# Reciprocal roots of the heads' variances: from three Newton steps on VectorE and GpSimd to logarithm, exponential and one Newton step

## The chip, the cores and the metric

The kernel runs on one core of one Trainium2 chip. The metric is the device time of one execution in microseconds (us), the median over several runs. The engines are TensorE (PE in the profile; PEld are its weight loads), VectorE (DVE), ScalarE (ACT), GpSimd (POOL) and SyncE (SP, which here only issues DMAs). An engine executes its own instructions in order and waits for the others by semaphores.

## The reference

Two layers act on x, of 4 batches x 256 tokens x 256 features. A layer is a gated cross attention to a context of 1601 tokens x 128 features, followed by a gated feed-forward part. The change lies in the attention of the first layer, which has 16 heads of 16 features. Queries and keys are normalised head by head before the scores:

```python
def _ln(t, w, b):
    m = jnp.mean(t, axis=-1, keepdims=True)
    v = jnp.var(t, axis=-1, keepdims=True)
    return (t - m) * jax.lax.rsqrt(v + EPS) * w + b

q = _ln((x @ Wq + bq).reshape(b, s1, H, HD), qn_w, qn_b)
k = _ln(kv[..., :HD], kn_w, kn_b)
ctx = _attn(qT, k, v) + _attn(qT, k_dca, v_dca)   # softmax over 1585 keys, and over the last 16 apart
x = x + jnp.tanh(g_xattn[0]) * (ctx @ Wo + bo)
```

So each token has one reciprocal root per head: 16 for a key token, 16 for a query token. The last 16 context tokens are a group of keys with norm weights of their own. The feed-forward part is a mixture of 16 experts in the first layer, and one with ternary weights in the second. They and the second attention aren't touched.

## The kernel before, in words

**Tiling.** Tokens lie on the 128 partitions. The 1585 main keys are 13 tiles of 128 tokens, prepared in five groups (three tiles each, the last of one). A group's keys are `kn`, 128 x 48 heads x 16 features; a batch's queries are `qraw`, 128 x 32 heads x 16. A variance tile has one column per head: 48, 32 or 16 of them.

**Preparing a group of keys.** `key_project` multiplies context by weights (L475); VectorE adds the bias into `kn` (L477), ScalarE copies the values into `vp` (L478). The mean is removed beforehand by centring the weights and biases (`center`). `scale_heads` then gives three steps: `square` on ScalarE (L379), `rsqrt`, and `scale`, in which GpSimd multiplies `kn` by the root (L388). `rsqrt` sums the squares and adds the epsilon on VectorE (L382, L383), makes a first guess with two integer instructions there (L365, L366), and runs three Newton steps of four instructions each on GpSimd (`pool_rsqrt`, L368 to L371), with the square's own buffer `sq` as work space. Then `split` writes the result as a sum of three bf16 parts: ScalarE rounds (L345, L349), GpSimd subtracts for keys and VectorE for queries (L346, L350). Last, SP transposes the parts into `kT` (L520). Queries go the same way, with their norm weights applied on VectorE (L544 to L551) and staged by GpSimd for each quarter of the heads (L616, L619).

**The loop.** A batch is four slabs of four heads, a slab is 14 slots. In each slot TensorE makes scores for the maxima (L647), whose maximum VectorE takes (L654), scores for the exponentials (L686), which ScalarE takes (L694), and multiplies with the values (L708). Between these, `plan_keys` and `plan_queries` place the steps of preparing the next batch at fixed slots: a step placed at slot n comes after the slot's own instructions on every engine. A group that begins at slot s has its square at s, `rsqrt` at s+1, `scale` at s+3, the two halves of the split at s+4 and s+6 and the transposes at s+7. This is done for batches 1, 2 and 3 while the batch before is attended to: 15 groups of keys and 3 of queries, 18 calls of `scale_heads`.

**The setup.** The first batch is prepared before the loop, with three larger roots in `deviations` (L829): two groups of keys and the queries together (128 columns), the rest of the keys (112), and the last tokens (16). They use `newton_rsqrt`, all on VectorE: two integer instructions (L356, L357) and three Newton steps of three (L359 to L361). The keys of this batch are in `kT`'s second buffer (`kn0`), multiplied by their root at L855.

**Order.** `keep_order` fixes the order of the instructions on each engine to the one in which they are written, so nothing moves past a waiting instruction.

Of the kernel before, what the change touches and what calls it, by code (L numbers as in the profile page):

```python
# [9 lines left out]
F32 = mybir.dt.float32  # L10
BF16 = mybir.dt.bfloat16
I32 = mybir.dt.int32
# [9 lines left out]
P = 128  # L22
# [26 lines left out]
def bc_last(ap, n):  # L49

    return ap.unsqueeze(2).to_broadcast([ap.shape[0], ap.shape[1], n])
# [8 lines left out]
def tile_gated_cross_blocks(ctx: ExitStack, tc: tile.TileContext, a: dict, out: bass.AP):  # L60
# [202 lines left out]
    with ExitStack() as ph:  # L263
# [12 lines left out]
        def load_group(b, gi):  # L276
# [4 lines left out]
            nc.sync.dma_start(out=t[:, :n], in_=a["ctxT"][:, b, k0 : k0 + n])  # L281
            return t

        wkv = wp.tile([P, 2 * D], F32, name="wkv")
        bkv = wp.tile([P, 2 * D], F32, name="bkv")
        nc.sync.dma_start(out=wkv[:, :D], in_=a["L0_xattn_Wk"])
# [64 lines left out]

            return [first, second]

        def newton_rsqrt(v, y, t):

            nc.vector.tensor_scalar(y.bitcast(I32), v.bitcast(I32), 1, None, ALU.arith_shift_right)  # L356
            nc.vector.tensor_scalar(y.bitcast(I32), y.bitcast(I32), -1.0, 1597463007.0, ALU.mult, ALU.add)  # L357
            for k in range(3):
                nc.vector.tensor_tensor(t, y, y, ALU.mult)  # L359
                nc.vector.scalar_tensor_tensor(t, t, -0.5, v, ALU.mult, ALU.mult)  # L360
                nc.vector.scalar_tensor_tensor(v if k == 2 else y, t, 1.5, y, ALU.add, ALU.mult)  # L361

        def pool_rsqrt(v, y, t):

            nc.vector.tensor_scalar(y.bitcast(I32), v.bitcast(I32), 1, None, ALU.arith_shift_right)  # L365
            nc.vector.tensor_scalar(y.bitcast(I32), y.bitcast(I32), -1.0, 1597463007.0, ALU.mult, ALU.add)  # L366
            for k in range(3):
                nc.gpsimd.tensor_tensor(t, y, y, ALU.mult)  # L368
                nc.gpsimd.tensor_tensor(t, t, v, ALU.mult)
                nc.gpsimd.tensor_scalar(t, t, -0.5, 1.5, ALU.mult, ALU.add)  # L370
                nc.gpsimd.tensor_tensor(v if k == 2 else y, t, y, ALU.mult)  # L371

        def scale_heads(src, n, g):

            sq = hp.tile([P, GN * H, HD0], F32, name="sq", bufs=1)
            v = small.tile([P, GN * H], F32, name="hn_var", bufs=2)[:n, :g]

            def square():
                nc.scalar.activation(sq[:n, :g], src, AF.Square)  # L379

            def rsqrt():
                nc.vector.reduce_sum(v, sq[:n, :g], axis=AX.X)  # L382
                nc.vector.tensor_scalar(v, v, 1.0 / HD0, 1e-6, ALU.mult, ALU.add)  # L383
                space = sq.rearrange("p g e -> p (g e)")[:n]
                pool_rsqrt(v, space[:, :g], space[:, g : 2 * g])

            def scale():
                nc.gpsimd.tensor_tensor(src, src, bc_last(v, HD0), ALU.mult)  # L388

            return [square, rsqrt, scale]  # L390


        bmask = wp.tile([P, HG], F32, name="bmask")
# [376 lines left out]
        def plan_keys(plan, b, base, at, l):  # L770

            ctxg, kns = {}, {}
            for gi, g in enumerate(groups):

                def fetch(gi=gi):
                    ctxg[gi] = fetched.pop((b, gi), None) or load_group(b, gi)

                place(plan, base + max(at[0][0], at[gi][0] - 8), [fetch])
                for i, slot in enumerate(at[gi]):
                    place(plan, base + slot, [lambda gi=gi, i=i: key_project(b, gi, ctxg[gi], kns, i)])  # L780

                def begin(gi=gi, slot=base + l[gi]):
                    steps = key_parts(gi, kns)
                    steps[0]()
                    for o, step in zip((1, 3, 4, 6), steps[1:]):
                        place(plan, slot + o, [step])
                    place(plan, slot + 7, [lambda: key_turn(b, gi)])

                place(plan, base + l[gi], [begin])
# [37 lines left out]
        def deviations(c0, c1):  # L827
            v = v0[:, c0:c1]
            nc.vector.tensor_scalar(v, v, 1.0 / HD0, 1e-6, ALU.mult, ALU.add)  # L829
            y, t = (lp.tile([P, NKT * H], F32, name=f"nr_{k}")[:, : c1 - c0] for k in "yt")  # L830
            newton_rsqrt(v, y, t)

        def square(t0, t1, base):

# [61 lines left out]
        first_pair(6, kn0)  # L896
        step(group[0])
        nc.vector.tensor_tensor(q3, q3, bc_last(v0[:, qcol : qcol + QT * H], HD0), ALU.mult)
        affine, fold, first_split, second_split = query_parts(0)[3:]
        affine()  # L900
        first_pair(8, kn0)
        step(group[0])
# [43 lines left out]
        for _ in last:  # L946
            pass
        nc.scalar.activation(gate, gate, AF.Tanh)
        early.close()
        ep = ph.enter_context(tc.tile_pool(name="l0e", bufs=4))  # L950

# [17 lines left out]
        for u, (b, s) in enumerate(slabs):  # L969
# [3 lines left out]
            if s == 0 and b + 1 < B:  # L973
                plan_keys(plan, b + 1, base_slot, KEYS[b > 0], PARTS_AT[b > 0])
                iterate(plan, base_slot + 32, last_tokens(b + 1), 12)
                if b == 0:
                    plan_queries(plan, 1, base_slot, [0, 3, 9, 10], [13, 14], [15, 16, 18, 19, 20, 21, 23])
                if b + 2 < B:
                    plan_queries(
                        plan, b + 2, base_slot + NS * SLOTS, [-8, -6, -4, -3], [-2, -1], [0, 1, 3, 4, 6, 8, 10]  # L980
                    )
            if s == 0 and b > 0:

# [665 lines left out]
```

## Time and profile before

| | |
|---|---|
| Median of 3 runs | 1640.45 us (1640.38 to 1642.27) |
| Profiled execution: its time, its span | 1644.6 us, 1642.8 us |
| PE busy | 1542.2 us (94%) |
| DVE busy | 1170.4 us (71%) |
| ACT busy | 788.0 us (48%) |
| POOL busy | 658.1 us (40%) |
| Chain that ended last, by engine | PE 77%, DVE 13%, ACT 3%, issue 2%, POOL 2% |
| Mean granted TensorE clock | 0.976 |

The span is the time from the first to the last instruction of one profiled execution; the table's shares are of that. The stages are: setup to 89 us, the first attention with preparation of the next batch to 492 us, its last batch to 603 us, and everything else (experts, second attention, second feed-forward part) after. A line of the groups has source line, engine, operation, output and inputs, shapes, count, busy time and mean duration, then the idle time of the engine ahead of them and who ended it. A line of the timeline has start and duration in us.

### The profile page before, as it was taken

To read this page: it belongs to the slowest core of one execution; us is meant where nothing else is said; L and a number is where in the kernel's file an instruction comes from. 1 tells how busy PE (TensorE), PEld (TensorE's weight loads), DVE (VectorE), ACT (ScalarE), POOL (GpSimd) and SP (SyncE) were. 2 spreads that over 40 slices of the span, in tenths; PEclk is the share of its full clock that TensorE was granted. 3 is DMA by queue.
4 is the path that set the end of the run, shared out by engine and by line. 5 is a ranking of instruction groups with operands and counts; after the bars stand their busy time and mean duration, and the time that the engine had idled before them with its cause. 6 is when DMAs were issued, how large, how long until landed. Compare 5 with 4: busy or idle time off the path is not lost.

```text
span 1642.8 us, 34188 instructions
## 1 busy us (share of the span) xinstructions
PE 1542.2 (94%) x13274; PEld 924.6 (56%) x13282; DVE 1170.4 (71%) x2621; ACT 788.0 (48%) x1808; POOL 658.1 (40%) x754
## 2 busy tenths in 40 slices
PE   4598899899999999998999999999999999999998
PEld 1254454454455554445666666666666666666665
DVE  6876668767767736677777777777877777877655
ACT  2144545554555553453555444544455444454443
POOL 4534414513621215534445444444445444444410
PEclk8699899999999999999999999999999999999999
DMA  3512612430424132000000000010000000000000
GB/s 102 100 35 45 94 32 45 78 57 16 87 44 95 37 90 110 1 2 2 15 9 21 9 15 15 8 21 3 15 9 15 15 15 15 9 2 2 2 0 27
DMA packets 148466, 54.06 MB, mean 33 GB/s; under 512 B 133200, under 2 KB 143952, under 8 KB 148176
## 3 DMA queue, kind: packets, MB, share of 16 engines
q1 hardware_dynamic: 134592, 50.65, 14.6%
q10 hardware_dynamic: 13712, 1.23, 0.6%
q8 instruction: 104, 1.70, 0.4%
q14 instruction: 58, 0.48, 0.1%
HBM read 24.30 MB, written 1.05 MB: 15 GB/s over the span
## 4 chain that ended last, share of the span: by engine, by line
PE 77%; DVE 13%; ACT 3%; issue 2%; POOL 2%; DMA 1%; ACTq 0%; SPq 0%; DVEq 0%; POOLq 0%
PE ps_o L1426 21%; PE ps_sc L1363 20%; PE ps_s L686 6%; PE ps_s L647 6%; PE ps_o L708 5%; DVE mxs L654 4%; PE ps_y L1444 4%; PE ps_m L1352 3%; PE ps_m L475 2%; PE ps_v L1186 2%; ACT pr L1378 1%; PE ps_a L1200 1%; PE ps_g L1557 1%; PE ps_x L1131 1%; PE ps_y L1582 1%
## 5 line engine op out<-in xcount | busy, mean ns | idle before, releaser
L1413 POOL TENSOR_TENSOR pr<-pr,rs 128x1604 f32<-128x1604 f32 x128 | 364.2, 2867 | 434.9 <-DMA rs<-ws 393.2
L1426 PE MATMUL ps_o<-pT,cx 128*128 128x256 f32 x1664 | 372.2, 381 | 7.8 <-DVE pT L1419 7.8
L1370 DVE CUSTOM_DVE_ANT_0 pr<-ps_sc,mk 128x401 f32<-128x401 f32 x512 | 294.6, 576 | 95.0 <-PE ps_sc L1363 56.2
L1363 PE MATMUL ps_sc<-ctxT,qT 128*32 128x401 f32 x4096 | 359.5, 502 | 0.4 <-DVE nm L1370 0.4
L1378 ACT ACTIVATE pr<-pr,nm 128x401 f32<-128x401 f32 x512 | 321.3, 629 | 71.0 <-DVE nm L1370 70.3
L1426 PEld LDWEIGHTS ps_o<-pT,cx 128*128 128x128 f32 x1664 | 318.0, 191 | 52.2 <-DVE pT L1419 8.5
L654 DVE TENSOR_REDUCE mxs<-ps_s 128x2 f32<-128x768 f32 (+1 forms) x256 | 245.9, 979 | 78.5 <-PE ps_s L647 77.9
L694 ACT ACTIVATE e<-ps_s 128x1024 f32<-128x1024 f32 (+1 forms) x224 | 214.7, 963 | 176.0 <-PE ps_s L686 161.5
L1419 DVE STREAM_TRANSPOSE pT<-pr 128x1664 f32<-128x1664 f32 x128 | 242.9, 1899 | 4.9 <-POOL pr L1413 4.7
L1363 PEld LDWEIGHTS ps_sc<-ctxT,qT 128*32 128x32 f32 x4096 | 126.2, 110 | 204.4 <-issue 119.5
L647 PE MATMUL ps_s<-kT,qTs 64*128 64x384 bf16 (+1 forms) x1536 | 177.6, 346 | 40.4 <-DMA qTs<-qp 18.1
L686 PE MATMUL ps_s<-qTs,kT 64*128 64x256 bf16 x2496 | 176.1, 272 | 11.0 <-DVE mxs L654 11.0
L686 PEld LDWEIGHTS <-kT 64*128 64x128 bf16 x2496 | 125.8, 95 | 57.5 <-issue 23.6
L647 PEld LDWEIGHTS <-qTs 64*128 64x128 bf16 x1536 | 67.0, 97 | 138.4 <-issue 91.4
L708 PE MATMUL ps_o<-e,vp 128*32 128x256 f32 x1664 | 112.8, 390 | 0.0
L1395 ACT ACTIVATE ws<-ws 32x32 f32<-32x32 f32 x64 | 14.6, 228 | 194.3 <-DVE ws L1394 194.3
L1436 ACT COPY ao<-ps_o 128x256 f32<-128x256 f32 x64 | 23.9, 373 | 152.5 <-PE ps_o L1426 141.3
L1378 ACT ACTIVATION_READ_ACCUMULATOR pr<-pr,nm 128x1 f32 x512 | 95.4, 186 | 0.0
L1444 PE MATMUL ps_y<-vo,ao 128*128 128x256 f32 x256 | 73.3, 409 | 2.1 <-ACT ao L1436 2.1
L1444 PEld LDWEIGHTS ps_y<-vo,ao 128*128 128x128 f32 x256 | 43.9, 191 | 46.5 <-ACT pr L1378 39.9
L708 PEld LDWEIGHTS ps_o<-e,vp 128*32 128x32 f32 x1664 | 44.6, 110 | 43.0 <-issue 25.6
L1352 PE MATMUL ps_m<-xnT,aq 128*128 128x256 f32 x256 | 65.8, 380 | 0.0
(288 smaller groups left out, 1553.9 us busy)
## 6 DMA issues: line engine op xcount, KB each, us to landing
ctxT<-in_ctxT_dram SPq DMA_DIRECT2D x4, 800.5 KB, 8.0
ctxg<-in_ctxT_dram SPq DMA_DIRECT2D x16, 192.0 KB, 3.2
kT<-in_L_xattn_Wq_dram SPq DMA_DIRECT2D x4, 512.0 KB, 3.5
wo<-in_L_xattn_Wo_dram SPq DMA_DIRECT2D x4, 512.0 KB, 4.5
bq<-nm SPq DMA_DIRECT2D x128, 2.0 KB, 1.7
bq<-nm ACTq DMA_DIRECT2D x128, 2.0 KB, 2.0
rs<-ws SPq DMA_DIRECT2D x128, 1.0 KB, 1.9
rs<-ws ACTq DMA_DIRECT2D x128, 1.0 KB, 1.8
```

The source lines that it names most:

```text
L647: nc.tensor.matmul(ps[:, k, :w], lhsT=qT[rows, j, i, r, :], rhs=kT[rows, 2 * s + r, c0 : c0 + w], start=j == 0, stop=j == NP - 1,)
L654: nc.vector.tensor_reduce(greatest_of[u][:, i, 2 * r : 2 * r + 2, n], ps[:, :, :w], AX.X, ALU.max)
L686: nc.tensor.matmul(ps[:, k, jj * S : (jj + 1) * S].rearrange("p (i q) -> p i q", i=QT), lhsT=kT[rows, 2 * s + r // 2, (j + jj) * P : (j + ...
L694: nc.scalar.activation(e[:, :, : nj * S], ps[:, :, : nj * S], AF.Exp)
L708: nc.tensor.matmul(summed[u][(r + k) * W : (r + k + 1) * W, :S], lhsT=vps[b % 2][:, j + jj, h * VW : h * VW + W], rhs=made[u, j, r][:, k, ...
L1363: nc.tensor.matmul(ps[i * TQ : (i + 1) * TQ, :KS], lhsT=queries[u][:, t * TQ : (t + 1) * TQ], rhs=ctxT[b][:, i * KS : (i + 1) * KS], start ...
L1370: nc.vector.tensor_tensor_reduce(out=prs[u % 3][:, t, :KS], in0=ps[:, :KS], in1=masks[b], scale=-1.0, scalar=3.0e38, op0=ALU.add, op1=ALU. ...
L1378: nc.scalar.activation(p, p, AF.Exp, bias=found[u][:, 0, t : t + 1], scale=-1.0, accum_out=found[u][:, 1, t : t + 1])
L1413: nc.gpsimd.tensor_tensor(p, p, bc_last(factors[:, ts], KS), ALU.mult)
L1419: nc.vector.transpose(pTs[u % 2][:, ts].rearrange("p t k -> p (t k)"), prs[u % 3][:, ts].rearrange("p t k -> p (t k)"))
L1426: nc.tensor.matmul(po[:, u % 2], lhsT=contexts[b][:, k, :], rhs=pTs[u % 2].rearrange("p t (k q) -> p t k q", q=TQ)[:, :, k, :], start=k == ...
L1444: nc.tensor.matmul(ys[b][:, i], lhsT=outs[u][:, i * P : (i + 1) * P], rhs=vo[:, h, :], start=(h, i) == (0, 0), stop=(h, i) == (H - 1, QT - 1),
```

## The change

The root becomes `exp(-0.5 * ln(v))` on ScalarE (`log_root`, two instructions), with one Newton step on VectorE after it (`newton`, three instructions). Both older helpers go. In `scale_heads` the step `rsqrt` is divided: `variance` at slot s+1 on VectorE, `root` at s+2 on ScalarE, and the Newton step at s+3 ahead of GpSimd's multiply. The work space is now two small tiles of their own, `hn_y` and `hn_t`, with one buffer each. ScalarE loads a table set that has both functions at the start of the program, and again after Tanh.

```diff
+        nc.scalar.preload_act_table_set("natural_log_exp_and_others")
         wkv = wp.tile([P, 2 * D], F32, name="wkv")
         bkv = wp.tile([P, 2 * D], F32, name="bkv")
         nc.sync.dma_start(out=wkv[:, :D], in_=a["L0_xattn_Wk"])
...
-        def newton_rsqrt(v, y, t):
-
-            nc.vector.tensor_scalar(y.bitcast(I32), v.bitcast(I32), 1, None, ALU.arith_shift_right)
-            nc.vector.tensor_scalar(y.bitcast(I32), y.bitcast(I32), -1.0, 1597463007.0, ALU.mult, ALU.add)
-            for k in range(3):
-                nc.vector.tensor_tensor(t, y, y, ALU.mult)
-                nc.vector.scalar_tensor_tensor(t, t, -0.5, v, ALU.mult, ALU.mult)
-                nc.vector.scalar_tensor_tensor(v if k == 2 else y, t, 1.5, y, ALU.add, ALU.mult)
-
-        def pool_rsqrt(v, y, t):
-
-            nc.vector.tensor_scalar(y.bitcast(I32), v.bitcast(I32), 1, None, ALU.arith_shift_right)
-            nc.vector.tensor_scalar(y.bitcast(I32), y.bitcast(I32), -1.0, 1597463007.0, ALU.mult, ALU.add)
-            for k in range(3):
-                nc.gpsimd.tensor_tensor(t, y, y, ALU.mult)
-                nc.gpsimd.tensor_tensor(t, t, v, ALU.mult)
-                nc.gpsimd.tensor_scalar(t, t, -0.5, 1.5, ALU.mult, ALU.add)
-                nc.gpsimd.tensor_tensor(v if k == 2 else y, t, y, ALU.mult)
+        def log_root(v, y):
+
+            nc.scalar.activation(y, v, AF.Ln)
+            nc.scalar.activation(y, y, AF.Exp, scale=-0.5)
+
+        def newton(v, y, t):
+
+            nc.vector.tensor_tensor(t, y, y, ALU.mult)
+            nc.vector.scalar_tensor_tensor(t, t, -0.5, v, ALU.mult, ALU.mult)
+            nc.vector.scalar_tensor_tensor(v, t, 1.5, y, ALU.add, ALU.mult)
 
         def scale_heads(src, n, g):
...
+            y, t = (small.tile([P, GN * H], F32, name=f"hn_{k}", bufs=1)[:n, :g] for k in "yt")
...
-            def rsqrt():
+            def variance():
                 nc.vector.reduce_sum(v, sq[:n, :g], axis=AX.X)
                 nc.vector.tensor_scalar(v, v, 1.0 / HD0, 1e-6, ALU.mult, ALU.add)
-                space = sq.rearrange("p g e -> p (g e)")[:n]
-                pool_rsqrt(v, space[:, :g], space[:, g : 2 * g])
+
+            def root():
+                log_root(v, y)
 
             def scale():
+                newton(v, y, t)
                 nc.gpsimd.tensor_tensor(src, src, bc_last(v, HD0), ALU.mult)
 
-            return [square, rsqrt, scale]
+            return [square, variance, root, scale]
...
-                    for o, step in zip((1, 3, 4, 6), steps[1:]):
+                    for o, step in zip((1, 2, 3, 4, 6), steps[1:]):
                         place(plan, slot + o, [step])
...
             y, t = (lp.tile([P, NKT * H], F32, name=f"nr_{k}")[:, : c1 - c0] for k in "yt")
-            newton_rsqrt(v, y, t)
+            log_root(v, y)
+            newton(v, y, t)
...
         nc.scalar.activation(gate, gate, AF.Tanh)
+        nc.scalar.preload_act_table_set("natural_log_exp_and_others")
...
-                    plan_queries(plan, 1, base_slot, [0, 3, 9, 10], [13, 14], [15, 16, 18, 19, 20, 21, 23])
+                    plan_queries(plan, 1, base_slot, [0, 3, 9, 10], [13, 14], [15, 16, 17, 18, 19, 20, 21, 23])
...
-                        plan, b + 2, base_slot + NS * SLOTS, [-8, -6, -4, -3], [-2, -1], [0, 1, 3, 4, 6, 8, 10]
+                        plan, b + 2, base_slot + NS * SLOTS, [-8, -6, -4, -3], [-2, -1], [0, 1, 2, 3, 4, 6, 8, 10]
```

One further line in the setup takes the queries' later steps from the fifth place of the list on, not the fourth.

More of the change, by code (lines that the diff above doesn't have):

```diff
@@ L898, in tile_gated_cross_blocks @@
         nc.vector.tensor_tensor(q3, q3, bc_last(v0[:, qcol : qcol + QT * H], HD0), ALU.mult)
-        affine, fold, first_split, second_split = query_parts(0)[3:]
+        affine, fold, first_split, second_split = query_parts(0)[4:]
         affine()
```

## The prediction

> **What bounds the kernel now.** I read the busy row and the chain that ended last first (TensorE 94% of the span, 77% of the chain), then cut the span by stage. The windows view, columns length, then busy time of PE, PEld, DVE, ACT, POOL, then granted clock, shows that the part the change touches isn't one regime:
>
> ```profile
> 23.50:50.30 26.80, 6.13 (x26) 2.15 (x25) 21.29 (x38) 7.96 (x12) 13.03 (x13) 0.64 0.33 60
> 50.30:68.20 17.90, 8.36 (x52) 3.98 (x50) 14.51 (x29) 4.53 (x7) 12.91 (x22) 0.69 0.61 98
> 89.00:218.00 129.00, 116.94 (x1310) 62.37 (x1312) 87.14 (x161) 68.15 (x100) 48.69 (x116) 0.95 0.31 52
> 492.00:603.00 111.00, 108.84 (x1546) 66.10 (x1542) 64.83 (x144) 63.30 (x78) 17.96 (x42) 1.00 0.29 68
> ```
>
> Until 89 us VectorE sets the pace (21.3 busy of 26.8). From 89 to 492 us, the loop in which the next batch's keys and queries are prepared, TensorE does, but is idle 33 of 403 us; from 492 us, where no keys are prepared, it is idle 2.2 of 111. What the change can win in the loop lies in those 33 us. After 603 us nothing it touches runs.
>
> The timeline of the setup has the first root. It stands on the chain with VectorE alone; ScalarE is idle from 21.69 to 27.63, GpSimd until 27.15:
>
> ```profile
> 23.31 0.23 DVE L829 TENSOR_SCALAR v<-v 128x128 f32<-128x128 f32 x1
> 23.57 0.23 DVE L356 TENSOR_SCALAR nr_y<-v 128x128 int32<-128x128 int32 x1
> ...
> 26.38 0.29 DVE L360 SCALAR_TENSOR_TENSOR nr_t<-nr_t,v 128x128 f32<-128x128 f32 x1
> 26.70 0.29 DVE L361 SCALAR_TENSOR_TENSOR v<-nr_t,nr_y 128x128 f32<-128x128 f32 x1
> ...
> 27.15 3.39 POOL L855 TENSOR_TENSOR kT<-kT,v 128x768 f32<-128x768 f32 x2 [14.78 <-DVE v L361]
> ```
>
> In the loop I listed every wait of TensorE and followed its releaser back. The longest, with brackets giving the idle time and who ended it:
>
> ```profile
> 161.14 0.29 POOL L371 TENSOR_TENSOR hn_var<-sq 128x48 f32<-128x48 f32 x1
> 161.36 0.21 POOL L616 MEMSET qp<- 128x24 bf16 x1
> 161.42 1.80 POOL L619 COPY qp<-qn 128x192 bf16<-128x192 bf16 x6
> 163.17 1.64 POOL L350 TENSOR_TENSOR kp<-kn,kp 128x768 bf16<-128x768 f32 x1
> ...
> 164.85 0.42 DVE L477 TENSOR_TENSOR kn<-ps_m,bkv 128x256 f32<-128x256 f32 x1 [5.74 <-POOL kp L350]
> ...
> 165.31 0.37 ACT L478 COPY vp<-ps_m 128x256 f32<-128x256 f32 x1 [5.97 <-DVE kn L477]
> ...
> 165.73 2.08 PE L475 MATMUL ps_m<-wkv,ctxg 128*128 128x512 f32 x2 [3.62 <-ACT vp L478]
> ```
>
> GpSimd's twelve root steps (157.30 to 161.43) hold back the split at L350, that the buffer `kn`, that VectorE, ScalarE and TensorE. The wait costs twice: the granted clock is 0.50 from 166 to 170 us and 0.73 from 170 to 172, so two matmuls of L475 take 2.08 instead of 1.12.
>
> **The change part by part.** ACT prices come from ACTIVATE rows: 228 ns at 32 columns, 408 at 256, so 0.8 ns a column: 241 ns at 48, 292 at 112, 305 at 128. A Newton instruction takes 0.29 at 128 columns and 0.17 at 16 (start to start 0.33 and 0.21), so at 48 about 0.24.
>
> *Setup roots.* At 128 columns eleven instructions, 23.57 to 26.99 (3.4 us), become two ACT and three DVE: 2 x 0.305 + 3 x 0.33 + three hand-overs of 0.03 = 1.7. Saved 1.7. VectorE's next instruction stands behind the Newton step and waits with it. The 112-column root (47.00 to 50.26) goes from 3.3 to 1.6: saved 1.7, ScalarE being idle from 45.18. The 16-column root (65.49 to 68.21) saves 1.6 of VectorE's time and nothing of the span: at 71.24 TensorE waits for the transposed `kp_last`, queued on SP behind six transposes of about 1.4 us issued from 59.3 on, and VectorE was itself only 0.33 us from waiting for it. Setup: -3.4.
>
> *Table loads.* The load moves from 9.76 us, where it followed ScalarE's DMA issues, to ahead of them, so these go out 1.3 us later. `wkv` then lands at 4.9, not 3.6; centring it takes 1.1 and is done before `x` lands at 7.5. The bias is centred at 8.8 and its transfer was issued by 2.2; the first copy of ScalarE starts at 11.06 either way. Cost 0; 1.3 if the cover fails, -0.5 if the `x` tiles land earlier without this traffic. The two loads around Tanh (2 x 1.283) lie in ScalarE's 13.36 us of idle before its first L694. Here a rule speaks against the change: the Trainium skill, "ScalarE: Activation LUTs", section "What ACT_TABLE_LOAD costs", adds a drain of about 1380 ns, 2.66 us a switch. The trace has the copy 0.02 us after its load (9.76 + 1.28, then 11.06), no drain. By the rule the pair costs 5.3, still inside the idle time, and the first transfers go out 2.7 late: `wkv` is centred at 7.4, still in time, and the first copy is 1.4 late. I take the row.
>
> *Loop.* Eighteen calls of `scale_heads`. GpSimd loses L368 to L371, 13.7 + 14.6 + 12.6 + 9.7 + 4.9 = 55.5 us. VectorE loses two integer steps (0.45 a call) and gains three (0.72): +0.27 a call, 4.9 in all. ScalarE gains 0.5 a call, 9. Moved: the multiply L388 followed GpSimd's chain as soon as that ended; now it waits for the Newton step two slots after the variance. A slot is 403/176 = 2.3 us, so it comes about as late as after the old chain (3.9 to 4.2 us). Behind the new waits: the logarithm waits for the variance issued a slot earlier, with the next slots' exponentials L694 behind it; Newton waits for ScalarE with the maxima L654 behind it. Each has a slot of lead. The ledger of TensorE's waits:
>
> - 165.73, 3.62: L350 needs only the copy ending at 158.35 and the staging, so it starts near 158.6, not 163.2; wait gone. Clock loss of 5.4 us at half speed gone too. -6.3.
> - 313.20 and 452.18, 1.78 each: ScalarE waits for L388, which stood behind GpSimd's roots, layernorm and staging. Without the roots it starts near 308, not 309.87. -1.8 each, -3.6.
> - 261.02 and 397.12, 2.8 each: VectorE's L549 took 1.98 instead of 0.67 while L388 ran (below). L388 now follows a Newton step that stands after L549. -1.3 each, and half of the 2.9 of half-speed clock that follows the second: -4.0.
> - 294.64 and 433.60, 1.0 each: L668 took 1.33 instead of 0.17 under L388, which moves behind it. -2.0.
> - 188.26, 2.34: one link is ScalarE's square waiting 1.37 for GpSimd. About -1.0, and half its 1.7 of slow clock: -1.8.
> - 148.74: 0.45 of integer steps less in front. -0.3.
>
> Sum -18.0. I give back a quarter (4.5), since engines that catch up show the wait behind, and charge a quarter (3.5) of the 13.9 us added to VectorE and ScalarE, as both are idle over a quarter of the loop; if all of it reached TensorE it would be 13.9. Loop: -10.0.
>
> The second rule that speaks against: "SBUF — State Buffer", section "SBUF: two separate sides": a VectorE instruction with two SBUF inputs and a GpSimd instruction reading SBUF exclude each other for a whole instruction. The trace agrees:
>
> ```profile
> 256.22 1.56 POOL L388 TENSOR_TENSOR kn<-kn,hn_var 128x768 f32<-128x768 f32 x1
> 256.34 1.98 DVE L549 TENSOR_TENSOR kb<-qraw,bc_L_xattn_kn_b 128x512 f32<-128x512 f32 x1
> ```
>
> L549 ends 0.54 us after L388. All three Newton instructions have two SBUF inputs, so a call that meets a GpSimd pass (1.5 to 1.65) can wait that long; at 48 columns by the row alone it is 0.72, by row and lock up to 2.4. In the order of the steps only the last group of the first prepared batch has such a pass in its slot; I add nothing beyond the charge.
>
> **Total.** -3.4 + 0 - 10.0 = -13.4. Against the profiled execution (span 1642.8, its time 1644.6) that is 1631.2; the median of the runs is 1640.45, 4 lower, which gives 1627.0. Bounds: -21.4 with nothing given back or charged (1619), -1.7 with the quarter given back, all added work on the path and a late start (-3.4 + 1.3 - 13.5 + 13.9: 1638.8).
>
> **The rivals.**
>
> - *Only the setup gains.* The waits are refilled by what stands behind them, since TensorE also waits for the maxima L654 13.3 us in sum in the loop. For: VectorE gains work. Against: the longest waits have GpSimd as their link. 1640.45 - 3.4 = 1637.0.
> - *All of it, and more clock.* Ledger in full: about 1619. For: the batch of 358.9 to 494.3 repeats the one before and took 2.9 us longer through one clock drop. Against: after a removed wait comes the next.
> - *The lock decides.* Newton meets GpSimd passes call after call, VectorE is late with L654 and TensorE waits. At 1.65 a hit and -13.4 - 3.5 otherwise, it needs more than ten hits in 18 that reach TensorE; with 15 the time is 1640.45 - 16.9 + 24.8 = 1648. Against: L350 of a group lies three slots behind its Newton step.
> - *It doesn't do what it says.* Logarithm and exponential in separate tables would reload at each call; the built instruction list has four loads in all, none in the loop. Left is no net effect, 1640.
>
> **How the numbers follow.** The forecast 0.58, more 0.12, setup only 0.18, no effect 0.03, the lock 0.09. A measurement here tells about 0.2% (3.3 us), so below 1637.2 is faster. Faster: 0.58 + 0.12 + half of 0.18 = 0.79; same 0.09 + 0.03 = 0.12; slower 0.09. The range reaches from the full ledger, 1618, to the late bound, 1639; the likeliest case alone is 1621 to 1634.
>
> **What would show it.** Right: first Newton step ends near 25.3, loop starts near 85.5; no table load between first L694 and SiLU; GpSimd's busy time near 603 us; no wait of 3.6 at a key projection; L549 at 0.7. Wrong: L694 waiting behind a logarithm, Newton instructions far above 0.3, first matmul or `x` later than now, a load with a drain, or new TensorE waits on L654 of over 10 us.

## The result and the profile after

| | before | after |
|---|---|---|
| Median of 4 runs each, compared on one chip | 1641.36 us (1640.38 to 1644.30) | 1620.10 us (1617.73 to 1622.86) |
| Ratio | | 0.9868, 95% interval 0.9847 to 0.9890 |
| Profiled execution: its time, its span | 1644.6, 1642.8 us | 1620.98, 1619.3 us |
| Mean granted TensorE clock | 0.976 | 0.981 |

The changed kernel is faster by 21.3 us; 13.4 was forecast. One profiled execution is unlike the timed ones: that of run e11, further down, had a mean granted clock of 0.556 and took 2611.82 us, so little more than VectorE's own durations is read from it. The line numbers of the changed kernel differ by a few: the key projection is L471, its bias and copy L473 and L474, the second half of the split L351, GpSimd's multiply L384, the folding of the query's bias L545, the maxima L643 and L650, the scores for the exponentials L682. Logarithm and exponential are L357 and L358, the Newton step is L362 to L364.

The busy row of the page, and its chain of work that ended last:

```profile
PE 1539.1 (95%) x13282; PEld 924.2 (57%) x13282; DVE 1159.3 (72%) x2615; ACT 798.9 (49%) x1852; POOL 601.7 (37%) x538
PE 80%; DVE 11%; ACT 3%; issue 3%; POOL 2%; DMA 1%; ACTq 0%; SPq 0%; DVEq 0%; POOLq 0%
```

GpSimd lost 56.4 us, as worked out (603 forecast). The row to stop at is VectorE's: it should have gained 4.9 us in the loop and lost some 6 in the setup, and has 11.1 less than before (1170.4). TensorE's share of the chain went from 77 to 80%, VectorE's from 13 to 11%.

**The setup.** The timeline of the changed kernel at its first root:

```profile
21.03 0.23 DVE L825 TENSOR_SCALAR v<-v 128x128 f32<-128x128 f32 x1
21.36 0.31 ACT L357 ACTIVATE nr_y<-v 128x128 f32<-128x128 f32 x1 [1.95 <-DVE v L825]
21.70 0.31 ACT L358 ACTIVATE nr_y<-nr_y 128x128 f32<-128x128 f32 x1
22.04 0.29 DVE L362 TENSOR_TENSOR nr_t<-nr_y 128x128 f32<-128x128 f32 x1 [0.78 <-ACT nr_y L358]
...
23.14 3.39 POOL L852 TENSOR_TENSOR kT<-kT,v 128x768 f32<-128x768 f32 x2 [10.82 <-DVE v L364]
```

From the variance to GpSimd's multiply it now takes 2.11 us (21.03 to 23.14) and took 3.84 (23.31 to 27.15): 1.73 saved, 1.7 forecast. The variance itself is 2.28 us earlier, which nothing in the forecast explains; more on that below.

**The loop.** The windows view over the whole loop, from the first key projection to the first matmul of the experts; columns are window, length, busy time of PE, PEld, DVE, ACT, POOL, granted clock, DMA share and GB/s. Before:

```profile
89.11:603.25 514.14, 479.18 (x5858) 266.46 (x5858) 350.32 (x668) 279.58 (x388) 169.74 (x410) 0.98 0.30 56
```

After:

```profile
81.29:575.40 494.11, 474.02 (x5858) 265.65 (x5858) 347.19 (x686) 285.22 (x424) 114.22 (x194) 0.99 0.32 58
```

The same 5858 matmuls take 20.0 us less. TensorE's idle time fell from 34.96 to 20.09 us (-14.9), and its busy time by 5.2, with a mean granted clock of 0.99 instead of 0.98. VectorE executes 18 instructions more and is busy 3.1 us less.

TensorE's waits in the loop, with columns for the sum in us, the number and the longest. Before, from 89 to 492 us:

```profile
PE ps_s L686 <- DVE mxs L654: 9.7, 19, 1.3
PE ps_m L475 <- ACT vp L478: 8.0, 4, 3.6
PE ps_m L475 <- DVE y L756: 5.5, 2, 2.8
PE ps_s L647 <- DVE mxs L654: 3.6, 4, 2.3
PE ps_s L647 <- ACT e L694: 3.6, 2, 1.8
```

After, from 80 to 500 us:

```profile
PE ps_s L682 <- DVE mxs L650: 8.2, 21, 1.2
PE ps_m L471 <- DVE y L752: 2.8, 2, 1.4
PE ps_s L643 <- DVE mxs L650: 2.6, 5, 1.1
PE ps_m L471 <- ACT vp L474: 2.3, 2, 1.9
PE ps_m L591 <- DVE pd L587: 2.0, 3, 1.5
PE ps_m L471 <- DVE mxs L650: 1.1, 1, 1.1
```

The key projection's wait for ScalarE's copy lost 5.7 us, the one for `y` halved, the one for the exponentials is gone. The waits of L682 and L643 for the maxima, which were to fill up again, became shorter too: over the whole loop (89 to 603 us before, 81 to 575 after) they sum to 15.3 us before and 12.4 after. (The 1.1 us in the last line stand ahead of the first key projection, at the end of the setup.) One wait grew, that of L591 for `pd`, from 0.5 to 2.0 us; it is taken up with the rivals at the end. The place of the longest wait, in the timeline of the changed kernel:

```profile
147.92 1.79 POOL L615 COPY qp<-qn 128x192 bf16<-128x192 bf16 x6
...
149.81 1.64 POOL L351 TENSOR_TENSOR kp<-kn,kp 128x768 bf16<-128x768 f32 x1
...
151.49 0.42 DVE L473 TENSOR_TENSOR kn<-ps_m,bkv 128x256 f32<-128x256 f32 x1 [0.94 <-POOL kp L351]
151.95 0.37 ACT L474 COPY vp<-ps_m 128x256 f32<-128x256 f32 x1 [1.31 <-DVE kn L473]
...
153.27 1.13 PE L471 MATMUL ps_m<-wkv,ctxg 128*128 128x512 f32 x2
```

VectorE waits 0.94 us for the split, not 5.74; the projection behind it stands without a bracket, so it doesn't wait, and it runs at 1.13 us, not 2.08.

### The profile page after: what moved, and what is told of

It reads as the page before. It is cut to its first block, busy times and chain, and to the rows that moved or that the text cites. A ratio compares the mean times of both kernels' runs of the same rounds, so it can differ in the third digit from the quotient of the medians.

```text
span 1619.3 us, 33935 instructions
## 1 busy us (share of the span) xinstructions
PE 1539.1 (95%) x13282; PEld 924.2 (57%) x13282; DVE 1159.3 (72%) x2615; ACT 798.9 (49%) x1852; POOL 601.7 (37%) x538
## 3 DMA queue, kind: packets, MB, share of 16 engines
q1 hardware_dynamic: 134592, 50.65, 14.9%
## 4 chain that ended last, share of the span: by engine, by line
PE 80%; DVE 11%; ACT 3%; issue 3%; POOL 2%; DMA 1%; ACTq 0%; SPq 0%; DVEq 0%; POOLq 0%
PE ps_o L1424 21%; PE ps_sc L1361 20%; PE ps_s L682 7%; PE ps_s L643 6%; PE ps_o L704 5%; PE ps_y L1442 4%; DVE mxs L650 4%; PE ps_m L1350 3%; PE ps_m L471 2%; PE ps_v L1184 2%; ACT pr L1376 1%; PE ps_a L1198 1%; PE ps_g L1555 1%; PE ps_x L1129 1%; PE ps_u L1555 1%
## 5 line engine op out<-in xcount | busy, mean ns | idle before, releaser
L650 DVE TENSOR_REDUCE mxs<-ps_s 128x2 f32<-128x768 f32 (+1 forms) x256 | 245.5, 979 | 75.8 <-PE ps_s L643 75.2
L643 PE MATMUL ps_s<-kT,qTs 64*128 64x384 bf16 (+1 forms) x1536 | 173.7, 339 | 33.3 <-DMA qTs<-qp 18.1
L682 PE MATMUL ps_s<-qTs,kT 64*128 64x256 bf16 x2496 | 173.6, 270 | 9.5 <-DVE mxs L650 9.3
L682 PEld LDWEIGHTS <-kT 64*128 64x128 bf16 x2496 | 125.0, 94 | 54.9 <-issue 21.7
L643 PEld LDWEIGHTS <-qTs 64*128 64x128 bf16 x1536 | 65.2, 96 | 128.7 <-issue 82.0
L1442 PEld LDWEIGHTS ps_y<-vo,ao 128*128 128x128 f32 x256 | 43.6, 190 | 46.3 <-ACT pr L1376 39.9
```

Of the source, the lines that this page charges most:

```text
L643: nc.tensor.matmul(ps[:, k, :w], lhsT=qT[rows, j, i, r, :], rhs=kT[rows, 2 * s + r, c0 : c0 + w], start=j == 0, stop=j == NP - 1,)
L650: nc.vector.tensor_reduce(greatest_of[u][:, i, 2 * r : 2 * r + 2, n], ps[:, :, :w], AX.X, ALU.max)
L682: nc.tensor.matmul(ps[:, k, jj * S : (jj + 1) * S].rearrange("p (i q) -> p i q", i=QT), lhsT=kT[rows, 2 * s + r // 2, (j + jj) * P : (j + ...
L1442: nc.tensor.matmul(ys[b][:, i], lhsT=outs[u][:, i * P : (i + 1) * P], rhs=vo[:, h, :], start=(h, i) == (0, 0), stop=(h, i) == (H - 1, QT - 1),
```

## The experiments

The gain of each is (1 - ratio) x 1642 us, with the interval worked out in the same way, because each experiment was timed beside its own runs of the kernel before (medians 1641.7 to 1642.7). The changed kernel itself has 21.7 (18.1 to 25.1) by that measure.

| Run | Median us | Ratio (95% interval) | Gain us |
|---|---|---|---|
| e1, setup roots only | 1637.86 | 0.9975 (0.9967 to 0.9983) | 4.1 (2.8 to 5.4) |
| e2, loop only | 1624.84 | 0.9889 (0.9874 to 0.9903) | 18.2 (15.9 to 20.7) |
| e3, table loads only | 1641.86 | 0.9993 (0.9985 to 1.0001) | 1.1 (-0.2 to 2.5) |
| e4, first load late | 1621.68 | 0.9872 (0.9860 to 0.9885) | 21.0 (18.9 to 23.0) |
| e5, Newton step twice | 1625.22 | 0.9896 (0.9883 to 0.9910) | 17.1 (14.8 to 19.2) |
| e6, logarithm twice | 1621.32 | 0.9871 (0.9858 to 0.9885) | 21.2 (18.9 to 23.3) |
| e7, three steps on VectorE | 1641.04 | 1.0004 (0.9996 to 1.0013) | -0.7 (-2.1 to 0.7) |
| e8, idle work on GpSimd | 1626.82 | 0.9912 (0.9898 to 0.9927) | 14.4 (12.0 to 16.7) |
| e9, no Newton step | 1616.35 | 0.9838 (0.9825 to 0.9852) | 26.6 (24.3 to 28.7) |
| e10, Newton step on GpSimd | 1623.66 | 0.9887 (0.9870 to 0.9903) | 18.6 (15.9 to 21.3) |
| e11, multiply's place only | 1642.87 | 1.0008 (1.0002 to 1.0015) | -1.3 (-2.5 to -0.3) |
| e12, e9 with the multiply's place | 1613.97 | 0.9830 (0.9817 to 0.9844) | 27.9 (25.6 to 30.0) |

### The two halves apart

The first run changes, in the kernel before, only the three roots of the setup and adds the two table loads:

```diff
+        nc.scalar.preload_act_table_set("natural_log_exp_and_others")
...
-            newton_rsqrt(v, y, t)
+            log_root(v, y)
+            newton(v, y, t)
...
         nc.scalar.activation(gate, gate, AF.Tanh)
+        nc.scalar.preload_act_table_set("natural_log_exp_and_others")
```

> Only the three large roots of the setup and the two table loads are changed; the eighteen calls in the loop keep their integer guess and GpSimd's three Newton steps. Theory A (the loop's gain comes from GpSimd's chain going, and the setup's gain is its own): about 7 below the kernel before, 1634 to 1637, with the first key projection of the loop near 81 to 83 us instead of 89.1, and the TensorE waits of 3.6 at 165 and 1.8 at 313 and 452 still there, earlier by that amount. Rival B (part of the loop's gain is only a shift of phase that an earlier start brings): those waits shrink here too and the time falls below 1630.

The second does the reverse, in the changed kernel:

```diff
-            log_root(v, y)
-            newton(v, y, t)
+            newton_rsqrt(v, y, t)
```

> Only the loop's calls and the two table loads are changed; the setup's three roots stay on VectorE with three Newton steps. Theory A: 16 to 19 below the kernel before, 1622 to 1625, and 3 to 5 above the changed kernel, with the loop beginning near 85 to 87 us. Rival B: about 1632, because the loop gains only half without the earlier start.

Measured: 4.1 us for the setup roots and 18.2 for the loop. The sum, 22.3, is the gain of the whole within its interval, so no dependence of the halves on each other is seen. The first run missed its range (1634 to 1637) from above: its loop began at 82.55 us, 6.6 earlier than in the kernel before, but only 4.1 of that are in the median. In the first, TensorE's loop waits are those of the kernel before (8.0 us on `vp`, longest 3.6; 5.6 on `y`); in the second they are those of the changed kernel. The rival that only the setup gains is dead, and the forecast's 3.4 for the setup stands; its 10.0 for the loop doesn't.

### The table loads

The loads alone, added to the kernel before:

```diff
+        nc.scalar.preload_act_table_set("natural_log_exp_and_others")
         wkv = wp.tile([P, 2 * D], F32, name="wkv")
...
         nc.scalar.activation(gate, gate, AF.Tanh)
+        nc.scalar.preload_act_table_set("natural_log_exp_and_others")
```

> The kernel before with the two table loads added and nothing else. If the load at the head of ScalarE's queue alone makes the first x tiles land earlier (through the order in which the first transfers are issued): layernorm statistics start near 6.4 us instead of 7.5, and the time is 1 to 2 lower, about 1639.5. If the earlier start of the changed kernel had another cause: statistics at 7.5 and 1641. If the loads cost anything on the path: above 1642.

The changed kernel with its first load behind the setup's first DMA issues:

```diff
-        nc.scalar.preload_act_table_set("natural_log_exp_and_others")
         wkv = wp.tile([P, 2 * D], F32, name="wkv")
...
+        nc.scalar.preload_act_table_set("natural_log_exp_and_others")
         early = ph.enter_context(ExitStack())
```

> The changed kernel with the first table load moved behind ScalarE's first nine transfers, where the kernel before has its load. If the early load brings the earlier start: the weight transfer goes out at 2.2 us as before, statistics start near 7.5, and the time is 1 to 2 above the changed kernel, about 1621.5. If it brings nothing: 1620.

Neither can be told from its neighbour: 1.1 us with an interval that holds 0, and 21.0 beside 21.7. No cost of the loads or of their place is seen. But what the forecast said of the DMA issues was only in part right, as the timeline of the changed kernel's ScalarE shows:

```profile
0.79 1.28 ACT L284 ACT_TABLE_LOAD   x1 [0.79 <-PEq L1636]
0.83 0.39 ACTq L288 DMA_DIRECT2D wkv<-in_L_xattn_Wv_dram  x1
...
1.73 0.45 ACTq L292 DMA_DIRECT2D bkv<-in_L_xattn_bv_dram  x1
...
4.92 0.39 ACTq L144 DMA_DIRECT2D w_wq<-in_L_xattn_Wq_dram  x1
...
66.88 0.27 ACT L436 COPY kdT<-ps_m 128x128 f32<-128x128 f32 x1 [7.07 <-PE ps_m L430]
67.17 1.28 ACT L945 ACT_TABLE_LOAD   x1
68.46 0.20 ACT L945 ACTIVATE gate<-gate 128x4 f32<-128x4 f32 x1
68.68 1.28 ACT L946 ACT_TABLE_LOAD   x1
80.33 1.02 ACT L690 ACTIVATE e<-ps_s 128x1024 f32<-128x1024 f32 x1 [10.36 <-DVE mxs L650]
```

In the kernel before, the weights of the query went out at 2.21 us:

```profile
2.21 0.46 ACTq L144 DMA_DIRECT2D w_wq<-in_L_xattn_Wq_dram  x1
```

ScalarE's first three issues go out at 0.83, 1.26 and 1.73 us, inside the load that lasts to 2.07: they aren't 1.3 us late, as forecast. The fourth is later than that, at 4.92 us, and at 5.51 in e3; in e4, with the load behind the issues, it is at 2.21 again. What it waits for isn't shown, and it cost nothing that the two medians can tell. Tanh's load starts 0.02 us after the copy ahead of it, Tanh 0.01 us after the load, and 10.36 us of idle time lie ahead of the first exponential.

### The price of added work

The Newton step of the loop done twice (`newton` has a fourth argument here, the tile for its result):

```diff
             def scale():
-                newton(v, y, t)
+                newton(v, y, t, y)
+                newton(v, y, t)
```

> The changed kernel with VectorE's Newton step run twice in each of the loop's 18 calls: 3 more instructions a call, 0.72 us by the row, 13 us of VectorE in all. Theory A with my charge of a quarter of added work: 3 slower than the changed kernel, 1623. If VectorE's added work is covered, as the changed kernel's time suggests: within 1.5, 1619 to 1622. If each Newton step meets GpSimd's passes (the lock rival): Newton instructions with means far above 0.25 us, and 8 to 20 slower.

Logarithm and exponential of the loop done twice:

```diff
             def root():
                 log_root(v, y)
+                log_root(v, y)
```

> The changed kernel with logarithm and exponential run twice in each of the loop's 18 calls: 2 more instructions on ScalarE, 0.5 us a call, 9 us in all. With a charge of a quarter: 2 slower, 1622. If ScalarE's work is covered: within 1, 1619 to 1621. If all of it reaches TensorE: 1629.

On VectorE, L362 to L364 are busy 22.4 us in the loop instead of 11.4. These 11.0 us cost 4.6 against the changed kernel's gain, 4.0 against the mean of e4 and e6, about 0.4 us for each (the intervals leave some 0.1 to 0.6). TensorE's waits from 78 to 500 us in e5:

```profile
PE ps_s L683 <- DVE mxs L651: 13.3, 26, 1.2
PE ps_s L644 <- DVE mxs L651: 4.4, 8, 1.8
```

That is 17.7 us where the changed kernel has 10.8: a late maximum is what VectorE's work costs. On ScalarE, 7.3 us more (busy 806.2 instead of 798.9) cost 0.5 us, less than the interval can tell from nothing. A quarter, as the forecast had it, lies within what is left open for VectorE; for ScalarE, whose measured price is 0.07, it looks too much.

### Where the work goes

No logarithm in the loop; two integer instructions and three Newton steps, all on VectorE, so GpSimd's chain is as gone as in the changed kernel:

```diff
             def root():
-                log_root(v, y)
+                pass

             def scale():
-                newton(v, y, t)
+                newton_rsqrt(v, y, t)
```

> The changed kernel, but in the loop the root is made on VectorE alone, with the integer guess and three Newton steps (11 instructions, all in the slot where the changed kernel has its one Newton step); no logarithm and exponential in the loop. GpSimd's chain is gone and its multiply sits where the changed kernel has it. Theory A (what counts is that GpSimd is free): most of the gain stays, 1621 to 1627, the rest being 8 more VectorE instructions of about 0.22 us a call, 32 us in all. Rival C (what counts is that VectorE's work stays small): 1632 or more.

The whole gain is lost, the setup's included. TensorE's waits in the loop of e7:

```profile
PE ps_s L691 <- DVE mxs L659: 19.8, 30, 1.9
PE ps_m L480 <- ACT vp L483: 5.6, 5, 1.9
```

The 3.6 us wait stayed away, but the root's instructions are 39.9 us of VectorE in the loop instead of 11.4, and these 28.5 us cost 22: 0.8 for each, twice the price of the eleven in e5. Whether the sum does it, or that all eleven instructions of a call stand in one slot, no run separates. The theory that freeing GpSimd makes the gain, whatever takes its work, falls here.

### GpSimd's free time

The changed kernel with twelve idle instructions on GpSimd behind each variance, about where the chain of roots was (55.5 us in all, as much as that chain; nothing waits for their result):

```diff
             def variance():
...
+                nc.gpsimd.tensor_tensor(z, v, v, ALU.subtract)
+                for k in range(11):
+                    nc.gpsimd.tensor_tensor(z, z, z, ALU.mult)
```

> The changed kernel with twelve GpSimd instructions of 48 columns after each variance that nobody needs (0.27 us each, 58 us in all, about what the old chain took, at the same place in GpSimd's order). Theory A, in the form that what stood behind the old chain on GpSimd's queue (staging, split, layernorm root) was what made TensorE wait: most of the loop's gain is lost, 1632 to 1638, and the wait of about 3.6 at a key projection near 158 us is back. Rival D (what counted was the root's own lateness, not the queue behind it): 1620 to 1625.

It takes 7.3 us of the gain away and lies between its two expectations. The long wait is back, as the timeline of e8 has it:

```profile
154.28 1.64 POOL L351 TENSOR_TENSOR kp<-kn,kp 128x768 bf16<-128x768 f32 x1
...
155.95 0.42 DVE L477 TENSOR_TENSOR kn<-ps_m,bkv 128x256 f32<-128x256 f32 x1 [5.17 <-POOL kp L351]
...
156.84 1.13 PE L475 MATMUL ps_m<-wkv,ctxg 128*128 128x512 f32 x2 [3.27 <-ACT vp L478]
```

The same chain as in the kernel before, link by link, 3.27 us instead of 3.62, and the clock falls to 0.57 behind it (158 to 162 us). The waits for the exponentials are back at 1.07 us each (1.78 before). What did not come back are the collisions: the folding took 0.68 us in e8 too, the maxima's last product 242 ns (443 before). So about 7 of the loop's 18 us go with GpSimd's free time, and the collisions went away for another reason. (The 7 are a net figure: the idle instructions also hold up VectorE's L362, 5.8 us in the loop instead of 3.8, and the longer wait for `pd` doesn't occur in e8.)

### The multiply's place

That reason is the place of the multiply behind the Newton step, which stands behind the folding on VectorE. Two runs move it. The first moves the Newton step to GpSimd, so that the multiply waits for nothing on VectorE:

```diff
             def scale():
-                newton(v, y, t)
+                nc.gpsimd.tensor_tensor(t, y, y, ALU.mult)
+                nc.gpsimd.tensor_tensor(t, t, v, ALU.mult)
+                nc.gpsimd.tensor_scalar(t, t, -0.5, 1.5, ALU.mult, ALU.add)
+                nc.gpsimd.tensor_tensor(v, t, y, ALU.mult)
```

> The changed kernel with the loop's Newton step as four small instructions on GpSimd, where the multiply stands, instead of three on VectorE. Theory B (each microsecond on VectorE costs about 0.35, GpSimd's free time is worth about 0.12 a microsecond, from 7.2 us lost by about 58 us of idle work): 12 us off VectorE gives 4.2 back, about 20 us more on GpSimd takes 2.5, so 1617.5 to 1619.5. Theory A (only GpSimd's free time counts): 2.5 slower, 1622 to 1624. If the multiply's place behind VectorE's Newton step was what kept it off the tail's folding and the maxima, L549's counterpart goes back toward 2 us and 443 ns shows again at the maxima, and the time is 1623 to 1627.

The second leaves the refinement out, in the loop and in the setup, so that the root is the rough one:

```diff
             def scale():
-                newton(v, y, t)
-                nc.gpsimd.tensor_tensor(src, src, bc_last(v, HD0), ALU.mult)
+                nc.gpsimd.tensor_tensor(src, src, bc_last(y, HD0), ALU.mult)
...
-            log_root(v, y)
-            newton(v, y, t)
+            log_root(v, v)
```

> The changed kernel with the Newton step left out everywhere, in the loop and in the three setup roots: the root is then the rough one of logarithm and exponential alone, a part of the computation that this kernel leaves out. Theory B (VectorE is the second bound, and each microsecond of it in the loop costs about 0.35): 18 calls lose about 11 to 13 us of VectorE's turns, 3.9 to 4.6 off the loop, and the setup loses two Newton steps of about 1.0 that stood in its chain, 1.5 to 2 off: 1614 to 1616. Theory A (GpSimd's free time alone made the gain, VectorE's load doesn't matter): only the setup's 1.5 to 2 come off, 1618.5 to 1619.5. Third reading (the slope of the run with the Newton step twice came from contention with GpSimd's passes, which one step already pays): less than the slope says, 1617 to 1618.

One slot of the second prepared batch shows all three cases. The changed kernel:

```profile
239.56 0.17 DVE L664 TENSOR_TENSOR mx<-mx,qp 128x8 f32<-128x8 f32 x1
...
240.93 0.68 DVE L545 TENSOR_TENSOR kb<-qraw,bc_L_xattn_kn_b 128x512 f32<-128x512 f32 x1
...
245.53 1.50 POOL L384 TENSOR_TENSOR kn<-kn,hn_var 128x768 f32<-128x768 f32 x1 [12.28 <-DVE hn_var L364]
```

The kernel with the Newton step on GpSimd (e10):

```profile
237.15 0.17 DVE L667 TENSOR_TENSOR mx<-mx,qp 128x8 f32<-128x8 f32 x1
...
238.39 1.67 POOL L387 TENSOR_TENSOR kn<-kn,hn_var 128x768 f32<-128x768 f32 x1
238.61 1.99 DVE L548 TENSOR_TENSOR kb<-qraw,bc_L_xattn_kn_b 128x512 f32<-128x512 f32 x1
```

The kernel without Newton step (e9):

```profile
237.76 1.50 POOL L383 TENSOR_TENSOR kn<-kn,hn_y 128x768 f32<-128x768 f32 x1 [8.60 <-DVE mx L661]
237.96 1.33 DVE L663 TENSOR_TENSOR mx<-mx,qp 128x8 f32<-128x8 f32 x1
...
240.49 0.68 DVE L544 TENSOR_TENSOR kb<-qraw,bc_L_xattn_kn_b 128x512 f32<-128x512 f32 x1
```

The VectorE instruction that starts while the multiply runs takes 1.99 us instead of 0.68, or 1.33 instead of 0.17, and ends 0.54 or 0.03 us behind it; the one that doesn't meet it takes its usual time. Behind the Newton step the multiply meets neither. In e10 VectorE lost the 11.4 us of the Newton step, worth 4 or more, and the kernel still became slower by about 3: by the price of e8 (7.3 for 55.5) the 19.7 us added to GpSimd would explain 2.6. TensorE's waits for `y`, behind the folding, rose from 2.8 to 4.5 us; those for the exponentials came back with 2.2 and those for `vp` rose from 2.3 to 3.9, as they did in e8 (2.1 and 5.6). So the place costs some of it and GpSimd's longer chain more than that price says; how much each, e10 doesn't tell, as its interval overlaps that of the changed kernel. The maxima, expected at 443 ns, stayed at 233. The theory that only GpSimd's time counts also contains the time of e10; it is e7 and e9 that speak against it. In e9 the Newton step's time is gained and a smaller part of it lost at the maxima (411 ns instead of 233), for 4.9 us net, of which an estimated 2 are the two Newton steps of 1.0 us that left the setup's chain. The other 3, for 9 us less on VectorE, are near the 0.4 for each of e5.

Is the place alone worth something? The next run is the kernel before, its roots where they were, in which the multiply reads a copy of the root made on VectorE:

```diff
             def scale():
+                r = small.tile([P, GN * H], F32, name="hn_r", bufs=1)[:n, :g]
+                nc.vector.tensor_scalar(r, v, 1.0, None, ALU.mult)
-                nc.gpsimd.tensor_tensor(src, src, bc_last(v, HD0), ALU.mult)
+                nc.gpsimd.tensor_tensor(src, src, bc_last(r, HD0), ALU.mult)
```

> The kernel before with its roots as they were, in which the multiply on GpSimd reads a copy of the root that VectorE makes in the step scale, so the multiply stands behind the fold and the maxima as it does behind the Newton step of the changed kernel; nothing else moves. If the multiply's place is a part of the gain of its own: the folding at 1.98 goes to 0.68 and the maxima at 443 ns to about 230, which the ledger put at 4.0 and 2.0, less about 1.5 for 18 copies on VectorE: 1636 to 1639 with the kernel before at 1642. If the place is worth something only once GpSimd has the free time (the later multiply delays the split behind it, with the roots still in the way): 1641 to 1645. The wait of 3.6 us at a key projection stays in both.

It is 1.3 us slower than the kernel before. The groups of VectorE in the loop of e11; columns after the shape are busy time, mean ns, idle time ahead and its releaser:

```profile
L389 DVE TENSOR_SCALAR hn_r<-hn_var 128x48 f32<-128x48 f32 (+2 forms) x17 | 4.1, 241 | 4.6 <-POOL hn_var L371 4.6
...
L551 DVE TENSOR_TENSOR kb<-qraw,bc_L_xattn_kn_b 128x512 f32<-128x512 f32 x3 | 2.1, 685 | 0.0
```

The folding is at 0.685 us, as expected, and the maxima's last product at 172 ns, so the collisions are gone, and still nothing is won. VectorE pays 4.1 us for the copies and stands 4.6 us waiting for the root's last step on GpSimd (L371), with its maxima queued behind. TensorE was busy for 807.5 of the 808 us from 92 to 900 in this execution, so what that wait costs at full clock can't be read from it. That the place is free only if the root is ready when VectorE comes to it, so that moving the multiply needs a freed GpSimd first, fits this, but is argued and not shown.

Last, both findings together, without the refinement but with the place (this root, too, is the rough one). The cut is against e9:

```diff
             def scale():
+                nc.vector.tensor_scalar(v, y, 1.0, None, ALU.mult)
-                nc.gpsimd.tensor_tensor(src, src, bc_last(y, HD0), ALU.mult)
+                nc.gpsimd.tensor_tensor(src, src, bc_last(v, HD0), ALU.mult)
```

> The kernel without any Newton step (the refinement of the roots is left out) in which the multiply reads a copy of the root made by VectorE in the step scale, so that it stands where the changed kernel has it. Against the run without Newton step, 1616.35: the maxima go from 411 ns back to about 230 (2.3 us of VectorE, 0.8 of the time at 0.35 a microsecond), 18 copies of about 0.2 add 3.6 (1.3): 1616 to 1617.5 if VectorE's load is all that counts. If the place is worth more than the time it saves on VectorE (a late maximum holds TensorE alone): 1613 to 1616. If nothing but the sum of small effects is at work, within 1 us of 1616.35.

The maxima are at 233 ns again and the copies cost 3.6 us. At 1613.97 us it is the fastest of all, 6 us below the changed kernel, but its interval overlaps that of e9, so whether the place is worth more than the copies here isn't settled. Of the unlike expectations it lies with the one that gives the place more than it saves on VectorE.

## Why the prediction was right in sign and too small in size

**Setup, -3.4: right.** e1 has -4.1 (-2.8 to -5.4), and both large roots saved 1.7 and 1.6 in the trace. The profile of the changed kernel seems to say more: the loop starts 7.8 us earlier. Of these, 2.28 were there before the first root. In the kernel before, four matmuls of the setup (L488, from 14.86 us) took 3.19 us under a lowered clock, and 1.88 in the changed kernel and in every other run compared. e4, whose DMA issues go out as in the kernel before, has them at 1.88 as well, so neither the load nor the order of the issues is the cause. e3, which keeps the old roots, begins its loop 2.6 us earlier too (86.51) at a median that can't be told from the kernel before. It looks like a draw of that one execution, and the medians of e1 are the better measure.

**Table loads, 0: right in the time, not in the detail** (above). The rule of the Trainium skill that was weighed there, "ScalarE: Activation LUTs", section "What ACT_TABLE_LOAD costs", with its drain of about 1380 ns, isn't borne out: 0.02 us lie ahead of Tanh's load and 0.01 us behind it, and e3's loads cost nothing that can be measured.

**Ledger of the loop, -18.0: right in sum, partly by luck.** e2 has -18.2. Item by item in the profiled executions:

| Item | Forecast | Measured | What the trace has |
|---|---|---|---|
| wait at 165.73, with its clock | -6.3 | -6.3 | gone, and 1.13 us for the two matmuls |
| 313.20 and 452.18 | -3.6 | -3.6 | no wait for the exponentials left |
| 261.02 and 397.12 | -4.0 | -5.7 | 2.8 became 1.4 twice; the whole 2.9 of clock came back |
| 294.64 and 433.60 | -2.0 | -1.5 | 1.02 became about 0.27 |
| 188.26 | -1.8 | +0.2 | 2.34 became 1.06 at 170.91 and, in a new collision, 1.49 at 176.55; the 1.7 of slow clock stayed |
| 148.74 | -0.3 | -0.3 | 2.29 became 1.95 |

That is -17.2 of the window's -20.0; the rest lies in waits outside the list, more than half of it in those for the maxima. Three items were off by 1.7, 0.5 and 2.0; in the sum that comes to 0.8, which the waits outside the list more than made up.

**"I give back a quarter (4.5)": this step failed.** On balance nothing was given back. The waits for the maxima, which were to take the gain over, fell from 15.3 us to 12.4 in the loop. One wait did take over, that for `pd` (below), with 1.5 us.

**"and charge a quarter (3.5)": mis-sized too, by how much isn't settled.** At the measured prices of 0.4 on VectorE (e5) and 0.07 on ScalarE (e6, not told from nothing) the added 4.9 and 9 us come to an estimated 2.6. If the ledger's 18.0 is taken as true, the interval of e2 (15.9 to 20.7) leaves at most 2.1 for it. VectorE's own busy time didn't rise at all: against the 4.9 stand the folding with 2.5 us less in the loop (4.6 to 2.1) and the maxima's last product with 2.3 less (5.3 to 3.0), and the windows show 3.1 less. That isn't a second gain, though. The savings are those of the four instructions that the ledger names at 261.02, 397.12, 294.64 and 433.60 (the third folding took 0.68 us in the kernel before as well), and it had credited them with 6.0 as waits of TensorE. Taken off the charge too, they would count twice.

Without the 4.5 the forecast would have been -17.9, without both deductions -21.4, against 21.3 measured (18.1 to 25.1 by the ratio). That the last is so near is partly luck, as the ledger's items show. It is the case given as "all of it, and more clock"; of the extra clock, the other half of the 2.9 behind 397.12 came, and the half of the 1.7 behind 188.26 that the ledger counted on did not.

**The rivals.** "The lock decides" needed Newton instructions that meet GpSimd's passes call after call: L362 to L364 average 212 ns in the loop, 359 at most. The rule of the Trainium skill behind it, "SBUF — State Buffer", section "SBUF: two separate sides", agrees with the rows of 1.99 and 1.33 us above, but the lock mostly worked for the change: it ended four collisions. It also made one that the forecast did not have. In the changed kernel the split of a group starts just ahead of the division of the last tokens' softmax (`pd`), an instruction with two inputs in SBUF:

```profile
174.57 1.64 POOL L351 TENSOR_TENSOR kp<-kn,kp 128x768 bf16<-128x768 f32 x1 [4.70 <-ACT kp L350]
174.82 1.67 DVE L587 TENSOR_TENSOR pd<-pd,d_sm 128x256 f32<-128x256 f32 x1
...
176.55 0.44 PE L591 MATMUL ps_m<-ident,pd 128*128 128x128 f32 x2 [1.49 <-DVE pd L587]
```

L587 takes 1.67 us instead of its usual 0.42, TensorE waits 1.49 us for it, and the granted clock is 0.64 and 0.51 in the two stretches of 2 us from 178 us on. In the kernel before, this split starts at 192.60 us, 0.02 us behind the end of the division. The mean of the division in the loop is 579 to 587 ns in every run with the new loop but e8, and 437 to 467 ns in e8 and in the kernels with the old loop (before, e1, e3; e11 not compared), so the new loop brings the collision. No run moves this split alone, so what that would be worth isn't measured.

**What is not settled.** Part of the gain of the profiled executions was given back after the loop. At the first token norm of the experts TensorE waits the same 1.5 us in both (1.48 at 615.23 us before, 1.47 at 587.40 after). Before, the clock stayed at 1.00; after, it was about 0.50 for some 10 us (588.4 to 598.4), which cost about 4. In the other runs' profiled executions, e11 aside, the same wait was followed by about 3 to 10 us near half clock, in all but e3 and e12. Since kernels with the loop of before and with that of after are on both sides, it looks like chance, but one trace of each can't show that.

## What to carry to other kernels

A deduction needs a place: here a quarter was given back without naming the wait that would take it, and none of that size did. Look for the engine whose work would refill a removed wait, and price its microseconds by a run that doubles one step (here about 0.4 on VectorE for 11, 0.8 over 28, nearly 0 on ScalarE). An instruction that moves may end locks and make new ones: list both, and credit an ended one once, as the wait it ends or as the engine's time. So the place of a long GpSimd pass among VectorE's two-input instructions deserves as much thought as its length.

## What the runs showed of the hardware that was not expected

- ScalarE's queue issues DMAs during a table load: the issues at 0.83, 1.26 and 1.73 us stand inside the load from 0.79 to 2.07. The next one went out at 4.92 us, against 2.21 without the load ahead of it; why isn't known.
- A TensorE wait of 1.5 us in a stretch of otherwise steady matmuls was followed by about 3 to 10 us near half clock in ten of thirteen profiled executions, and by none in three (the kernel before, e3 and e12). So a removed wait can be worth more than its length, but need not be in every execution.
- Four matmuls of the setup took 3.19 us in the one profile of the kernel before and 1.88 in the changed kernel, e1, e2, e3, e4 and e9: a stage's gain read off two single traces carries such draws, and here it made 7.8 us out of about 4.
